# A graph-attention kernel on one core: the last slot as a routine of its own, the first loads in pieces, and the projection's products ahead of q's in the second slot

## The chip, the cores and the metric

The kernel runs on one core of one Trainium2 chip. The metric is the device time of one execution in microseconds (us), lower is better. Times are given as the median of several runs; a profiled execution is one run more, with its own time. Engines are called by the profile's names: PE (TensorE), DVE (VectorE), ACT (ScalarE), POOL (GpSimd), SP (SyncE, which here only issues DMAs); PEld is PE's loading of stationary operands.

## What is computed

Thirty-two graphs of 512 nodes with 512 features each go through two layers. Everything is fp32.

```
x: (32, 512, 512)   adj: (32, 512, 512)
# layer 0: attention with 8 heads of 64, weighted by adj, then residual and layer norm
q, k, v = x @ Wq.T + bq, x @ Wk.T + bk, x @ Wv.T + bv
attn = softmax(q k^T / 8 + log(clip(adj, 1e-8)))
x = layer_norm(x + (attn v) @ Wo.T + bo) * gamma + beta
# layer 1: graph attention with one head
p = x @ fc_w.T + fc_b
l = (p . q_w + q_b) + (p . k_w + k_b)^T ;  l = l + (1 - adj) * (-1e9) ;  l = leaky_relu(l)
out = softmax(l) p + x
```

## The kernel before

**Batches and slots.** The function `fast` works on one graph (batch b) after another. A batch has four slots p = 0 to 3, one for each pair of heads, written by `slot(b, p)`. In each slot PE makes the pair's scores (`score`, L701; ACT takes the exponential, L706), DVE multiplies with the adjacency (`factors`, L714) and adds up the columns (`sums`, L724, L727), and PE multiplies with v (`values`, L739, one slot later). Round this core lies the other work of three batches: q and k of the next pair (`seven_qk`, L540), v of the next batch (`seven_v`), the output projection Wo of the batch before (`seven_wo`, L188) with its layer norm, and layer 1 of the batches before (`dots`, `k_rows`, `softmax`, `eT`, `z`, `out_units`). The q/k, v and Wo products are made with seven half-size products in place of eight (a Strassen-like scheme), so their sums use the same PSUM bank more than once: a bank gets product 1, DVE reads it, and product 6 is added on top.

**Order.** The program order on PE, DVE, ACT and SP is the order in which the code calls things (`manual_schedule`); each engine works through its own queue in that order and waits with semaphores. POOL isn't in that list; it only adds the bias bo to n (L473). So a step that waits holds up all that stands behind it on its engine.

**The second slot (p = 1)** holds, for the batch before, the scaling of the attention's outputs oT 2 and 3 with the reciprocal sums (`scale`, L794), `third_difference` (L808), then four units of `seven_wo` alternating with the units of `seven_qk(b, 2)`, q first, with the second half of `sums` between. Unit 0 of Wo is products 1 and 5, after which DVE writes two differences (L657) and adds bank a to n (L658); unit 1 is products 2 and 6; product 6 is added to bank a. At the slot's start `load_again(b - 1)` fetches x of the batch before as n, and POOL adds bo to it.

```
for i in range(4):
    run(next_qk[i : i + 1])
    if i == 0:
        sums(b, p, 1)
    run(units[i : i + 1])
```

**The start.** x of batch 0, the weights (each one DMA of 1 MB on SP's queue) and the adjacency (16 DMAs) are loaded; PE transposes x (L271), makes q, k and all four units of v, and then enters slot (0, 0). `fold_units` prepares constants of layer 1 in three steps spread over batch 0: `bias` in slot (0, 1), `offset` in (0, 2), `spread` at the end of (0, 3) (L254 to L259). `combine` prepares the sums of weights for the seven products.

**The end.** In slot (31, 3) `load_again(31)`, `load_last_e` (the last adjacency, plain), two leftover `out_units` of batch 29 and `divide_here` (sums over partitions on PE, L817, reciprocals by logarithm and exponential on ACT, refined on DVE, L827 to L833). After the loop stands a tail with layer 1 of batch 30 and what is left of batch 31, ending with `find_range` (a check of the sums' range, L855 to L871) and the outputs.

Of the kernel before, what the change touches and what calls it, by code (L numbers as in the profile page):

```python
# [19 lines left out]
P = 128  # L20
# [10 lines left out]
def kernel(  # L31
# [72 lines left out]
    def load_weight(w, name):  # L104
        w_sb = const.tile([P, DC, D], FP, name=name)
        nc.sync.dma_start(out=w_sb, in_=w.rearrange("(c p) o -> p c o", p=P))
        return w_sb
# [11 lines left out]
    def load_b(dst, src):  # L119
        nc.sync.dma_start(out=dst, in_=src.rearrange("(c p) d -> p c d", p=P))  # L120
# [22 lines left out]
    def load_first_constants():  # L143
        K["wq"] = load_weight(wqT, "wq")
        K["bq"] = load_col(const, bq, "bq")
        K["wk"] = load_weight(wkT, "wk")
        K["bk"] = load_col(const, bk, "bk")
        K["wv"] = load_weight(wvT, "wv")
# [45 lines left out]
    def fold_units(psum, scratch):  # L194
# [56 lines left out]
        def spread():  # L251
            for _, _, part, dg, name, b0 in vectors:
                ps = psum.tile([P, D], FP, tag="m", name=f"ps_{name}")
                nc.tensor.matmul(ps, ones, dg, start=True, stop=True)  # L254
                nc.vector.tensor_copy(K[name], ps)
                ps = psum.tile([P, D], FP, tag="m", name=f"ps_{name}_part")
# [82 lines left out]
    def dots_units(s, small, junk, name):  # L339
# [3 lines left out]
        def unit(c):  # L343
            n = s["n"][:, c, :]
            for u, to in ((K["uk"], s["k"]), (K["uq"], s["q"])):
                nc.vector.scalar_tensor_tensor(  # L346
                    junk, n, 1.0, u, ALU.mult, ALU.mult, accum_out=to[:, c : c + 1]
                )

        def biases():  # L350
            nc.vector.tensor_scalar_add(s["k"], s["k"], K["k0"])
            nc.vector.tensor_scalar_add(s["q"], s["q"], K["q0"])
        return [lambda c=c: unit(c) for c in range(NC)] + [biases]
# [50 lines left out]
    def residual(s):  # L404

        def over(row):
            return row.unsqueeze(1).to_broadcast([P, NC, D])
        nc.vector.tensor_mul(s["yb"], s["n"], over(K["gamma"]))
        nc.vector.tensor_add(s["yb"], s["yb"], over(K["cc"]))
# [9 lines left out]
    def out_units(s, dst, psum, name):  # L419
        def unit(c):  # L420
            pg = psum.tile([P, D], FP, tag="m", name=f"pg_{name}_{c}")
            product(pg, lambda i: s["zT"][:, i, ts(c, P)], lambda i: K["fc"][:, i, :])
            o = s["yb"][:, c, :]
            nc.vector.scalar_tensor_tensor(o, pg, s["r"][:, c : c + 1], o, ALU.mult, ALU.add)  # L424
            nc.sync.dma_start(out=dst[ts(c, P), :], in_=o)
        return [lambda c=c: unit(c) for c in range(NC)]


    def fast(ctx):
# [10 lines left out]
        def load_x(b):  # L440
            s = S[b]
            if b == 0:
                s["n"] = act.tile([P, NC, D], FP, tag="n", name=f"n_{b}")
                load_b(s["n"], x[b])
# [30 lines left out]
        def load_last_e():  # L475
            S[B - 1]["e"] = cT
            load_b(cT, adj[B - 1])
# [6 lines left out]
        def xT(b):  # L484
            s = S[b]
            s["xT"] = act.tile([P, DC, N], FP, tag="xT", name=f"xT_{b}")
            if b == 0:
                return transpose_units(s["n"], s["xT"], ps_m, nc.scalar.copy, f"x_{b}")
            return transposes(s["xT"], s["x"])

# [319 lines left out]
        def divide_here(b, p):  # L810
# [4 lines left out]
            ps = ps_m.tile([P, N], FP, tag="m", name=f"ps_{b}_{p}")  # L815
            for j in range(2):
                nc.tensor.matmul(  # L817
                    ps[j * DK : (j + 1) * DK, :], ones[:, :DK], s["as", p][:, j, :],
                    start=True, stop=True,
                )  # L820
            i = 2 * B - 1 + p % 2
            R = act.tile([P, 2, N], FP, tag="R", name=f"t_{b}_{p}")
            t, r = R[:, 0, :], R[:, 1, :]
            junk = S[b - 1]["w"][:, 0, :]
            nc.scalar.activation(r, ps, AF.Ln)
            nc.scalar.activation(r, r, AF.Exp, scale=-1.0)
            nc.vector.tensor_mul(t, ps, r)  # L827
            nc.vector.scalar_tensor_tensor(
                junk, ps, SUM_MAX, t, ALU.is_le, ALU.mult, accum_out=seen[:, i : i + 1]
            )  # L830
# [382 lines left out]
```

## Time and profile before

| | us |
|---|---|
| median of 3 runs (lowest, highest) | 3574.13 (3572.62, 3574.59) |
| the profiled execution | 3570.67 |
| its span, first to last instruction | 3568.5 |
| PE busy | 3510.2 |
| DVE busy | 2872.7 |
| ACT busy | 1277.6 |
| start of slot (31, 3) | 3439.12 |
| first product of z of batch 31 | 3533.29 |

The granted clock of PE was 0.995 over the span. One batch takes 108.86 us in the middle of the run (the first L658 of batch 3 starts at 361.2 us, that of batch 30 at 3300.0). In a row of the timeline the first two numbers are start and duration in us, "x8" counts instructions, and what stands in brackets is the idle time of the engine ahead of it and what ended it. PE is pipelined, and the ends of its instructions are modelled, so neighbours overlap by some 0.07 to 0.2 us; distances are best read from start to start.

### The profile page before, as it was taken

The numbers are of one execution on the slowest core, as the hardware profiler recorded it, in microseconds if no ns is written. First come the engines' busy times: TensorE is split into PE (matmuls) and PEld (weight loads), VectorE is DVE, ScalarE is ACT, GpSimd is POOL, SyncE is SP. The second block draws the span as 40 slices with busy tenths as digits, with TensorE's granted clock in tenths as the row PEclk, the third lists the DMA queues.
The fourth block names the chain that finished last, engine by engine and source line by source line (L and its number), as shares of the span: only waits on it lengthen the run. The fifth ranks groups of instructions, "written<-read, shape, count | busy, mean of one in ns | idle before, by whom it ended". The sixth has DMA issues, their size and how long they took to land.

```text
span 3568.5 us, 38741 instructions
## 1 busy us (share of the span) xinstructions
PE 3510.2 (98%) x13826; PEld 2040.4 (57%) x13826; DVE 2872.7 (80%) x4708; ACT 1277.6 (36%) x2060; POOL 201.7 (6%) x137
## 2 busy tenths in 40 slices
PE   9999999999999999999999999999999999999988
PEld 3555655655655555556656555555566565565544
DVE  5788878787888888787888888887878888888874
ACT  3334333333333333333343333333333433333332
POOL 0000000000000000000000000000000000000010
PEclk9999999999999999999999999999999999999999
DMA  4344323344233443233442324432334423344220
GB/s 112 48 74 87 54 69 71 66 86 72 60 75 60 80 87 57 68 72 63 86 82 50 75 61 80 86 57 70 74 62 84 86 46 74 65 76 87 51 69 27
DMA packets 880223, 250.68 MB, mean 70 GB/s; under 512 B 807068, under 2 KB 807068, under 8 KB 880024
## 3 DMA queue, kind: packets, MB, share of 16 engines
q1 hardware_dynamic: 880024, 248.15, 35.0%
q8 instruction: 110, 1.80, 0.2%
q14 instruction: 89, 0.73, 0.1%
HBM read 181.93 MB, written 34.65 MB: 61 GB/s over the span
## 4 chain that ended last, share of the span: by engine, by line
PE 95%; DVE 3%; ACT 1%; DMA 0%; issue 0%; SPq 0%; DVEq 0%; ACTq 0%
PE f L540 19%; PE sc L701 13%; PE po L739 12%; PE pz L278 12%; PE pg L278 12%; PE pw_a L188 5%; PE pv_a L188 4%; PE pw_c L188 3%; PE pw_b L188 3%; PE pv_c L188 3%; PE pv_b L188 3%; PE pq L540 2%; PE ps L756 2%; ACT at L706 1%; DVE w L346 0%; DVE at L714 0%
## 5 line engine op out<-in xcount | busy, mean ns | idle before, releaser
L706 ACT ACTIVATE at<-sc 128x1024 f32<-128x1024 f32 x512 | 496.5, 1022 | 892.6 <-PE sc L701 891.3
L714 DVE SCALAR_TENSOR_TENSOR at<-cT,at 128x1024 f32<-128x1024 f32 x512 | 618.3, 1249 | 181.4 <-ACT at L706 181.4
L701 PE MATMUL sc<-qT,kT 64*128 64x512 f32 x2048 | 509.4, 616 | 3.8 <-DVE qT L564 1.9
L739 PE MATMUL po<-at,v 128*64 128x512 f32 x2048 | 469.1, 600 | 1.0 <-DVE at L714 0.9
L278 PE MATMUL pg<-fc,zT 128*128 128x512 f32 x1024 | 445.3, 592 | 1.7 <-DVE yb L424 1.7
L278 PE MATMUL pz<-eT,n 128*128 128x512 f32 x1024 | 446.4, 593 | 0.0
L473 POOL TENSOR_TENSOR n<-n,bo 128x512 f32<-128x512 f32 x128 | 200.7, 1597 | 3262.5 <-PE po L739 1535.8
L701 PEld LDWEIGHTS sc<-qT,kT 64*128 64x128 f32 x2048 | 176.1, 186 | 299.0 <-issue 264.5
L278 PEld LDWEIGHTS pg<-fc,zT 128*128 128x128 f32 x1024 | 194.3, 190 | 234.0 <-issue 217.4
L278 PEld LDWEIGHTS pz<-eT,n 128*128 128x128 f32 x1024 | 195.2, 191 | 230.5 <-issue 220.7
L727 DVE TENSOR_TENSOR as<-as,at 128x1024 f32<-128x1024 f32 x256 | 314.0, 1226 | 5.6
L739 PEld LDWEIGHTS po<-at,v 128*64 128x64 f32 x2048 | 135.7, 137 | 319.2 <-issue 315.0
L540 PE MATMUL f<-T,qk_s 128*128 128x256 f32 x992 | 247.4, 382 | 7.0 <-DVE T L521 3.9
L416 ACT COPY zT<-pz 128x512 f32<-128x512 f32 x128 | 75.0, 586 | 429.3 <-PE pz L278 429.3
L540 PEld LDWEIGHTS f<-T,qk_s 128*128 128x128 f32 x992 | 181.0, 190 | 43.4 <-ACT at L706 5.8
L540 PE MATMUL f<-xT,wq 128*128 128x256 f32 x744 | 194.9, 385 | 8.2 <-ACT at L706 8.2
L747 ACT COPY oT<-po 128x512 f32<-128x512 f32 x128 | 75.2, 588 | 321.6 <-PE po L739 321.6
L540 PEld LDWEIGHTS f<-xT,wq 128*128 128x128 f32 x744 | 137.8, 190 | 53.4 <-ACT at L706 33.9
L724 DVE TENSOR_TENSOR as<-at,at 128x1024 f32<-128x1024 f32 x128 | 154.1, 1204 | 2.2
L794 DVE TENSOR_TENSOR oT<-oT,R 128x512 f32<-128x512 f32 x126 | 128.5, 1061 | 7.5 <-DMA R<-d 7.5
L540 PE MATMUL f<-xT,qk_s 128*128 128x256 f32 x496 | 127.3, 379 | 0.0
L540 PE MATMUL f<-T,wk 128*128 128x256 f32 x496 | 127.3, 379 | 0.0
(212 smaller groups left out, 4710.6 us busy)
## 6 DMA issues: line engine op xcount, KB each, us to landing
n<-in_x_dram SPq DMA_DIRECT2D x32, 1024.0 KB
cT<-in_adj_dram SPq DMA_DIRECT2D x512, 64.0 KB
out_dram<-yb SPq DMA_DIRECT2D x128, 256.0 KB
R<-d SPq DMA_DIRECT2D x126, 256.0 KB
x<-in_x_dram SPq DMA_DIRECT2D x124, 256.0 KB
e<-in_adj_dram SPq DMA_DIRECT2D x31, 1024.0 KB
eP<-e SPq DMA_DIRECT2D x480, 64.0 KB
w<-dk SPq DMA_DIRECT2D x32, 256.0 KB
```

The source lines that it names most:

```text
L188: nc.tensor.matmul(to[:, n, :], right(i, c)[:, ts(n, P)], left[i][:, c, :], start=(first and n == 0 and c == 0), stop=(n == KH - 1 and c = ...
L278: nc.tensor.matmul(ps, lhs(i), rhs(i), start=(i == 0), stop=(i == 3))
L473: nc.gpsimd.tensor_add(s["n"][:, c, :], s["n"][:, c, :], K["bo"])
L540: nc.tensor.matmul(to, left[i][:, c, ts(p, P)], s["B"][i][:, c, :], start=(first and c == 0), stop=(c == KH - 1), skip_group_check=True,)
L701: nc.tensor.matmul(sc[:, j, :], s["kT", p][rows, ts(kc, P)], s["qT", p][rows, :], start=True, stop=True,)
L706: nc.scalar.activation(at, sc, AF.Exp, scale=SCALE)
L714: nc.vector.scalar_tensor_tensor(at, cT[:, kc, :].unsqueeze(1).to_broadcast([P, 2, N]), ADJ_MIN, at, ALU.max, ALU.mult,)
L724: nc.vector.tensor_add(s["as", p], s["at", p, 0], s["at", p, 1])
L727: nc.vector.tensor_add(s["as", p], s["as", p], s["at", p, kc])
L739: nc.tensor.matmul(s["po", p][j * DK : (j + 1) * DK, :], s["v"][h // 4][:, kc, ts(h % 4, DK)], s["at", p, kc][:, j, :], start=(kc == 0), s ...
L747: nc.scalar.copy(s["oT"][p], s["po", p])
L794: nc.vector.tensor_mul(oT, oT, s["R", p][:, k, :])
```

## The change

- **Start:** x of batch 0 and wq come in four DMAs each; `first_xT` transposes x piece by piece into four PSUM banks, and the copies alternate between ACT and DVE. Two of v's four units move behind the q and k products of slot (0, 0). In batch 0 `bias` stands behind all q and k products of its slot, half of wv's combination and all of wo's move, and `spread` moves from the end of slot (0, 3) to slot (1, 0), with both big products ahead of both small ones.
- **Second slot, every batch from 1 on:** the second half of `sums` first, then each unit of `seven_wo` ahead of the unit of `seven_qk` with the same number.
- **Dots:** k's dots and q's are separate lists, in the third slot taken two and two.
- **Last slot:** `last_slot` takes the place of slot (31, 3) and the tail, with a new order of all that is in them; `divide_here` is three steps (add, invert, refine) with banks of the scores' kind; `residual` can work on some of the four rows; `find_range` is two steps, put between z's units; n of batch 31 is loaded in slot (31, 2).

The diff, cut to its core:

```diff
-    def load_weight(w, name):
+    def load_weight(w, name, pieces=1):
-        nc.sync.dma_start(out=w_sb, in_=w.rearrange("(c p) o -> p c o", p=P))
+        load_b(w_sb, w, pieces)
         return w_sb
...
-    def load_b(dst, src):
-        nc.sync.dma_start(out=dst, in_=src.rearrange("(c p) d -> p c d", p=P))
+    def load_b(dst, src, pieces=1):
+        n = 4 // pieces
+        for i in range(pieces):
+            nc.sync.dma_start(
+                out=dst[:, ts(i, n), :],
+                in_=src[ts(i, n * P), :].rearrange("(c p) d -> p c d", p=P),
+            )
 
...
-        K["wq"] = load_weight(wqT, "wq")
+        K["wq"] = load_weight(wqT, "wq", 4)
...
         def spread():
-            for _, _, part, dg, name, b0 in vectors:
+            for _, _, _, dg, name, _ in vectors:
                 ps = psum.tile([P, D], FP, tag="m", name=f"ps_{name}")
                 nc.tensor.matmul(ps, ones, dg, start=True, stop=True)
                 nc.vector.tensor_copy(K[name], ps)
+            for _, _, part, _, name, b0 in vectors:
                 ps = psum.tile([P, D], FP, tag="m", name=f"ps_{name}_part")
                 nc.tensor.matmul(ps[:, :DC], ones, part, start=True, stop=True)
                 nc.vector.tensor_reduce(extra[:, 0:1], ps[:, :DC], AX.X, ALU.add)
...
+        def dot(c, u, to):
+            nc.vector.scalar_tensor_tensor(
+                junk, s["n"][:, c, :], 1.0, u, ALU.mult, ALU.mult, accum_out=to[:, c : c + 1]
+            )
+
+        def bias(to, b0):
+            nc.vector.tensor_scalar_add(to, to, b0)
+        ks = [lambda c=c: dot(c, K["uk"], s["k"]) for c in range(NC)]
+        qs = [lambda c=c: dot(c, K["uq"], s["q"]) for c in range(NC)]
+        return ks + [lambda: bias(s["k"], K["k0"])], qs + [lambda: bias(s["q"], K["q0"])]
...
+    def residual(s, cs=slice(0, 4)):
-            return row.unsqueeze(1).to_broadcast([P, NC, D])
-        nc.vector.tensor_mul(s["yb"], s["n"], over(K["gamma"]))
-        nc.vector.tensor_add(s["yb"], s["yb"], over(K["cc"]))
+            return row.unsqueeze(1).to_broadcast([P, cs.stop - cs.start, D])
+        nc.vector.tensor_mul(s["yb"][:, cs, :], s["n"][:, cs, :], over(K["gamma"]))
+        nc.vector.tensor_add(s["yb"][:, cs, :], s["yb"][:, cs, :], over(K["cc"]))
...
+        ps = {}
+
+        def mul(c):
+            ps[c] = psum.tile([P, D], FP, tag="m", name=f"pg_{name}_{c}")
+            product(ps[c], lambda i: s["zT"][:, i, ts(c, P)], lambda i: K["fc"][:, i, :])
+
+        def add(c):
             o = s["yb"][:, c, :]
-            nc.vector.scalar_tensor_tensor(o, pg, s["r"][:, c : c + 1], o, ALU.mult, ALU.add)
+            nc.vector.scalar_tensor_tensor(o, ps[c], s["r"][:, c : c + 1], o, ALU.mult, ALU.add)
             nc.sync.dma_start(out=dst[ts(c, P), :], in_=o)
-        return [lambda c=c: unit(c) for c in range(NC)]
+        return [(lambda c=c: mul(c), lambda c=c: add(c)) for c in range(NC)]
...
-                load_b(s["n"], x[b])
+                load_b(s["n"], x[b], 4)
...
+        def first_xT():
+
+            s = S[0]
+            s["xT"] = act.tile([P, DC, N], FP, tag="xT", name="xT_0")
+            pt = [ps_m.tile([P, N], FP, tag="m", name=f"pt_x_{i}") for i in range(3)]
+            pt.append(ps_o.tile([P, N], FP, tag="po", name="pt_x_3"))
+            for c in range(NC):
+                for i in range(DC):
+                    nc.tensor.transpose(pt[i][:, ts(c, P)], s["n"][:, c, ts(i, P)], ident)
+            for i in range(DC):
+                (nc.scalar.copy, nc.vector.tensor_copy)[i % 2](s["xT"][:, i, :], pt[i])
...
+            ps = ps_s.tile([P, 2, N], FP, tag="s", name=f"ps_{b}_{p}")[:, 0, :]
+            i = 2 * B - 1 + p % 2
+            R = act.tile([P, 2, N], FP, tag="at", name=f"t_{b}_{p}", bufs=6)
+            t, r = R[:, 0, :], R[:, 1, :]
+
+            def add():
+                for j in range(2):
+                    nc.tensor.matmul(
+                        ps[j * DK : (j + 1) * DK, :], ones[:, :DK], s["as", p][:, j, :],
+                        start=True, stop=True,
+                    )
+
+            def invert():
+                nc.scalar.activation(r, ps, AF.Ln)
+                nc.scalar.activation(r, r, AF.Exp, scale=-1.0)
+
+            def refine():
+                junk = S[b - 1]["w"][:, 0, :]
+                nc.vector.tensor_mul(t, ps, r)
+                nc.vector.scalar_tensor_tensor(
+                    junk, ps, SUM_MAX, t, ALU.is_le, ALU.mult, accum_out=seen[:, i : i + 1]
                 )
+                nc.vector.scalar_tensor_tensor(t, t, 2.0, r, ALU.subtract, ALU.mult)
+                oT = s["oT"][p]
+                nc.vector.scalar_tensor_tensor(oT, oT, -1.0, t, ALU.mult, ALU.mult)
+            return add, invert, refine
...
+            def over_elements():
+                ...
+                pf = ps_m.tile([P, 512], FP, tag="m", name="pf")
+                nc.tensor.transpose(pf[:2, :P], low, ident)
+                nc.vector.tensor_reduce(least, pf[:2, :P], AX.X, ALU.min)
+
+            def over_partitions():
+                one = ps_m.tile([P, 512], FP, tag="m", name="one")
+                nc.tensor.transpose(one[:1, :2], least, ident[:2, :2])
+                ...
+            return over_elements, over_partitions
...
                 if b == 0:
-                    run(combine(K["wv"], K["v_s"]) + combine_qk()[:1])
+                    run(combine(K["wv"], K["v_s"])[:1] + combine_qk()[:1])
                 run(next_qk)
-                units = z(b - 2) if b >= 2 else []
+                units = z(b - 2) if b >= 2 else [spread] if b == 1 else first_v[2:]
                 run(units[:2])
...
                 run(units[2:])
+                if b == 0:
+                    run(combine(K["wv"], K["v_s"])[1:])
...
             if p == 1:
-                units = seven_wo(last, long_banks(last)) if last >= 0 else [bias]
-                for i in range(4):
-                    run(next_qk[i : i + 1])
-                    if i == 0:
-                        sums(b, p, 1)
-                    run(units[i : i + 1])
-                if last >= 0:
+                sums(b, p, 1)
+                if last < 0:
+                    run(next_qk)
+                    bias()
+                else:
+                    units = seven_wo(last, long_banks(last))
+                    for i in range(4):
+                        run(units[i : i + 1])
+                        run(next_qk[i : i + 1])
                     run(stats_units(S[last], small, last))
                     mask(S[last])
             if p == 2:
+                if b == 0:
+                    run(combine(K["wo"], K["wo_s"]))
                 run(next_qk)
...
+                outs = out_units(S[b - 2], out[b - 2], ps_m, b - 2) if b >= 2 else []
                 if b == B - 1:
-                    units, rest = units[:2], units[2:]
-                run(units[:1])
-                dot = dots(last) if last >= 0 else []
-                run(dot[:2])
-                run(units[1:2])
-                run(dot[2:])
+                    load_again(b)
+                    outs, rest = outs[:2], outs[2:]
+                if b == 0:
+                    offset()
+                run_out(outs[:1])
+                ks, qs = dots(last) if last >= 0 else ([], [])
+                run(ks[:2] + qs[:2])
+                run_out(outs[1:2])
+                run(ks[2:] + qs[2:])
                 if last >= 0:
                     k_rows(last)
                 if b < B - 1:
                     sums(b, p, 1)
-                run(units[2:])
+                run_out(outs[2:])
                 divided(b, 0)
                 if b == 0:
-                    run(combine_qk()[1:] + combine(K["wo"], K["wo_s"]))
+                    run(combine_qk()[1:])
...
+        def last_slot():
+            b, last = B - 1, B - 2
+            muls, adds = [m for m, _ in rest], [a for _, a in rest]
+            for kc in (0, 1):
+                score(b, 3, kc)
+            run(values(b, 2))
+            factors(b, 3, 0)
+            sums(b, 3, 0)
+            for kc in (2, 3):
+                score(b, 3, kc)
+            factors(b, 3, 1)
+            load_last_e()
+            vs = values(b, 3)
+            vs[0]()
+            run(muls[:1])
+            run(softmax(last))
+            run(adds[:1])
+            vs[1]()
+            here2, here3 = divide_here(b, 2), divide_here(b, 3)
+            here2[0]()
+            run(muls[1:])
+            nc.vector.tensor_add(S[b]["as", 3], S[b]["as", 3], S[b]["at", 3, 2])
+            run(adds[1:])
+            nc.vector.tensor_add(S[b]["as", 3], S[b]["as", 3], S[b]["at", 3, 3])
+            scale(b, 0)
+            first_difference(b)
+            here2[1]()
+            run(eT(last))
+            for u in here3[:2]:
+                u()
+            here2[2]()
+            here3[2]()
+            zs = z(last)
+            zs[0]()
+            wos = seven_wo(b, other_banks(b))
+            run(wos[:2])
+            new_yb(last)
+            residual(S[last], slice(0, 1))
+            residual(S[last], slice(1, 2))
+            third_difference(b)
+            wos[2]()
+            residual(S[last], slice(2, 3))
+            residual(S[last], slice(3, 4))
+            wos[3]()
+            invert(S[last])
+            run(stats_units(S[b], small, b))
+            run(zs[1:])
+            norm = normalise_units(S[b], small, b)
+            norm[0]()
+            mask(S[b])
+            run(norm[1:])
+            ks, qs = dots(b)
+            run(ks)
+            k_rows(b)
+            run(qs)
+            outs = out_units(S[last], out[last], ps_m, last)
+            soft = softmax(b)
+            run_out(outs[:1])
+            outs[1][0]()
+            soft[0]()
+            outs[1][1]()
+            outs[2][0]()
+            soft[1]()
+            outs[2][1]()
+            run_out(outs[3:])
+            rest_of_layer1(b)
+            zs = z(b)
+            run(eT(b) + zs[:1])
+            range_steps = find_range()
+            range_steps[0]()
+            zs[1]()
+            flag = range_steps[1]()
+            run(zs[2:])
+            run_out(out_units(S[b], out[b], ps_m, b))
+            return flag
...
-        run(xT(0) + qk(0, 0) + v(0))
+        first_xT()
+        first_v = v(0)
+        run(qk(0, 0) + first_v[:2])
...
                 if b == B - 1 and p == 3:
-                    load_again(b)
-                slot(b, p)
-        last = B - 1
...
+                    flag = last_slot()
+                else:
+                    slot(b, p)
         return flag
```

## Prediction, made before the changed kernel was run

> **What bounds the kernel now.** The page first: TensorE (PE) is busy for 98% of the span, and the chain that ended last lies 95% on it.
>
> ```profile
> PE 3510.2 (98%) x13826; PEld 2040.4 (57%) x13826; DVE 2872.7 (80%) x4708; ACT 1277.6 (36%) x2060; POOL 201.7 (6%) x137
> PE 95%; DVE 3%; ACT 1%; DMA 0%; issue 0%; SPq 0%; DVEq 0%; ACTq 0%
> ```
>
> So what can be won is PE's idle 58 us, and what can be lost is any new wait of PE, above all one that repeats with the batch. Next the windows: from 300 to 3400 us PE idles about 0.3 us per batch, and its waits there have one entry, `f L540 <- ACT at L706`, 29 times 0.27 us (second slot, q's products wait for score banks). The other idle time lies at the ends: 6.5 us for the first x, about 12 between 90 and 200 us, and this in the end piece (PE's waits from 3439 us; columns: total, times, longest):
>
> ```profile
> PE ps L817 <- DVE as L727: 7.6, 1, 7.6
> PE pt_e L271 <- ACT cT L396: 7.0, 4, 6.3
> PE pt_e L271 <- ACT e L396: 5.9, 4, 5.2
> PE pg L278 <- DVE yb L424: 1.7, 1, 1.7
> PE po L739 <- DVE at L714: 0.9, 1, 0.9
> ```
>
> Then the one slot that every batch repeats and the change reorders, the second (here batch 20; start, duration), DVE first:
>
> ```profile
> 2196.08 2.36 DVE L714 SCALAR_TENSOR_TENSOR at<-cT,at 128x1024 f32<-128x1024 f32 x2 [5.55 <-ACT at L706]
> 2198.48 1.23 DVE L724 TENSOR_TENSOR as<-at,at 128x1024 f32<-128x1024 f32 x1
> 2199.62 3.45 DVE L794 TENSOR_TENSOR oT<-oT,R 128x512 f32<-128x512 f32 x2
> 2202.99 2.90 DVE L808 TENSOR_TENSOR oT<-oT,oT 128x256 f32<-128x256 f32 x2
> 2205.82 2.35 DVE L714 SCALAR_TENSOR_TENSOR at<-cT,at 128x1024 f32<-128x1024 f32 x2
> 2208.09 0.41 DVE L549 TENSOR_TENSOR qT<-f,qT 128x256 f32<-128x256 f32 x1
> 2208.42 2.47 DVE L727 TENSOR_TENSOR as<-as,at 128x1024 f32<-128x1024 f32 x2
> 2210.81 0.75 DVE L657 TENSOR_TENSOR oT<-oT,t 128x256 f32<-128x256 f32 x2
> 2211.48 0.68 DVE L658 TENSOR_TENSOR n<-pw_a,n 128x512 f32<-128x512 f32 x1
> ```
>
> and PE in the same slot:
>
> ```profile
> 2210.39 1.89 PE L188 MATMUL pw_b<-wo,oT 128*128 128x256 f32 x8
> 2212.22 1.99 PE L188 MATMUL pw_a<-wo_s,oT 128*128 128x256 f32 x8
> ...
> 2220.18 1.13 PE L701 MATMUL sc<-qT,kT 64*128 64x512 f32 x4
> ```
>
> The slot's first score starts at 2193.85; I count from there. DVE has no gap from +2.2 to the end of L658 at +18.31, and PE's product 6 (second pw_a) starts at +18.37, 0.06 after L658's end: it adds to the bank that L658 reads. PE would have been ready at about +18.27. So this place is already on the edge of DVE. The slot ends (next score) at +26.33.
>
> **What the Trainium skill says.** "PSUM — Partial Sum Buffer", PSUM bank collisions: two engines may not be in one bank at once, so software must wait; that is the 0.06 us order above, and it stays. "SBUF — State Buffer", Who interferes with whom: a DVE instruction with two SBUF inputs contends with a GpSimd instruction that reads SBUF. The trace agrees: during GpSimd's four adds n+bo (2199.55 to 2205.61) L794 and L808 take 3.45 and 2.90 us; without them two such scalings took 1.29 (3454.20) and two differences of that shape, L802, 0.75 (3455.41). "TensorE: Matmul & The Clock Gate", Part 1: after an idle window of about 3.4 us, free-running, PE's clock halves. Here four products took 2.05 instead of 1.03 us after a wait of 2.44 us (94.63), but 1.13 after 2.41 (198.52), 1.10 after 1.44: near 2.4 us it is chance, below 1.7 it was never seen.
>
> **1. Second slot, batches 2 to 31.** Removed: the 0.27 us wait for score banks, since Wo's products 1 and 5 need only oT scaled a slot earlier. Moved: q's unit (four products of 0.86) falls behind Wo's first unit, and a second q unit (1.73) falls behind product 6. PE is then ready for product 6 after 1.92+3.58+1.92 (scores, values, scores), 3.45 (Wo 1, 5), 3.45 (q), 1.73 (Wo 2) = +16.05, with 0.1 for the change of form +16.15, instead of +18.27. DVE's queue ahead of L658 loses one instruction only, L549 (0.33 start to start): everything else, the sums L727 too, still stands ahead, and its start hangs on the exponentials of the slot's first scores. L658 ends at +17.98, product 6 starts at +18.04: a new wait of 1.9 us. Behind it on PE: product 6 1.73 (+0.1 as now), q 1.73, Wo 4, 3 3.45, k 0.86, Wo 7 1.73, form 0.08 = 9.68, next score at +27.72. I look for a second wait: k's last add (L568) ends near +26.7, before +27.72; product 4's bank is free at +19.6, needed at +21.5. None. Cost **+1.4 us per batch** (+1.2 if the 0.1s vanish), 30 times: **+42**. GpSimd's load of n is issued where it was, so nothing moves it. In batch 1 n isn't loaded and GpSimd adds nothing there; DVE is early enough, no loss.
>
> **2. The start and batches 0, 1.** x in four pieces: first q product near 7.5 instead of 9.61 (last piece at 6.35 as now, four transposes 0.8, copies on two engines). But wq ends and wk follows at the rate seen (380 GB/s: 2.76 us per MB), wk lands near 11.9, so k starts there instead of 13.05: 1.15 won. Six more DMA issues at 0.5 us push the adjacency's issues 3.1 us back, landing 25.4 instead of 22.3; its reader starts by 26.1, before 32.5 now, since the scores come before half of v; covered. v's second half hides the 0.78 wait at 42.45, bias behind k the 0.84 at 61.28: slot (0,2) starts at 58.0, not 61.28. Then DVE rules: bias 10.2 and factors 4.6 from 58.0, wo's combination (2.65, moved into DVE's gap) to 75.5, then xT, at 76.86 now. From there to the add L549 before at 102.86 it was 26.4 with the combination in it, now 23.8: PE's product there starts at 99.3 instead of 103.32. spread leaves slot (0,3): 111.19 to 117.23, 6.0 with its 2.99 wait. So 10.0 at slot (1,0). There DVE runs without a gap to the copy of uq (about 125.8), next slot 126.0 instead of 135.0: **9.0 won**, less 1 for a clock drop at one of the new waits of up to 2.6: **-8** (5 to 10).
>
> **3. The end.** n(31) is loaded a slot earlier: issue 3432.2, landing +5.6 as in batch 4's second slot, GpSimd's adds 3437.9 to 3443.9 lie on the dots of slot (31,2) (two SBUF inputs, 1.68 instead of 0.69), so DVE's factors start at 3447.6, not 3444.4: PE waits 2.25 for them. PE from 3439.12 to the last z(30): scores 3.84, values 7.43, pg 6.9, sums 1.9, transposes 3.4, pz 13.75, Wo 12.1 = 49.3, with that wait and 1.15 for the third difference (DVE's queue from the softmax at 3456.5 to it sums to 23.3, so 3479.8) 52.7: 3491.85. The waits of 7.6 and 5.9 are gone, covered by pg, transposes and z. Now ACT copies zT first (0.7), then the normalising factors 1.5, mask 1.15, four k dots 3.05, turn 0.2: 3498.45; round trip of the k row 5.75 (3516.43 to 3522.23 before): 3504.2; softmax to first pz 11.06 (3522.23 to 3533.29 before): 3515.3, 18.0 earlier. q's dots and pg (to 3506.4) lie beside it. Last: find_range's first step now stands on PE behind the first pz. It needs the residual (4.57 after the out DMA, 2.2) and seven small DVE steps, low at 3520.7, pz ends at 3518.75: 1.95 of wait and 0.4, against 0.88 now: 1.4 back. **-16.6** (10 to 22).
>
> **Costed at nothing.** The k dots ahead of q's and the split of out_units into product and add issue the same instructions in nearly the same places while q's and k's results are needed only after both. The second half of wv's combination waits for v's products in batch 0, 0.68 us in a stretch where DVE waits for exponentials (4 us ahead of its old place at 47.05); without that cover 0.7 once. On SP, n(31)'s load stands ahead of the k row's and the output's DMAs and waits for the last q products (3432.2), all of those come after 3437; the reload of cT stands ahead of one output and waits for the last factors (3453.4), and its reader comes 40 us later. The row of reciprocals for oT 0 and 1 lands 9.6 us after its issue began (3444.48 to 3454.1 before), now about 3457.2, its scaling comes at 3462.8: if DVE were earlier, this would be late next.
>
> **Sum.** 42 - 8 - 16.6 = +17.4 on the profiled execution's 3570.67 (span 3568.5 and 2.17 around it): 3588. The median of the runs shown is 3.46 above it, so **3591**.
>
> **Rivals.** (a) Faster: product 6 doesn't wait, because DVE gets to L658 by +16.1. Against it: DVE's queue has no gap. For it: GpSimd's adds cost DVE 4.3 us in this slot, and were they to fall elsewhere DVE would be there. Then 30 x -0.28 = -8.4 and 3574 - 8.4 - 8 - 16.6 = 3541. The sign turns where the slot costs 24.6 / 30 = 0.8, that is L658 0.6 earlier than I say; chance 0.13, and 0.06 for between, near 3572. (b) The new wait of 1.9 halves the clock each time: 1.8 more (2.05 + 1.80 against 1.03 twice at 94.63), 30 times 54: 3645. Only waits over 2.4 did so here: 0.07. (c) The end gains a third: DVE, whose queue there has no slack, is later by what GpSimd and the split residual cost, -6: 3602; chance 0.12. (d) Likeliest, 0.62: 3591, own range 3580 to 3603.
>
> **Numbers.** A measurement tells about 0.2%, 7 us, from no change: 3567 to 3581 is the same. Faster 0.15 (a and part of between), same 0.10 (the low edge of d and between), slower 0.75. Range 3570 to 3613: (d), (c), most of between, with the start's and the end's bounds; (a) and most of (b) left out.
>
> **What would show it.** A wait `pw_a L188 <- DVE n L658` of about 1.9 us, 30 times, and none of f on `at L706`; batch period 110.25 instead of 108.86; slot (1,1) near 126; z(31) starting 18 us before the old place, counted from slot (31,3). Wrong if the period falls, or the products behind L658 run at half clock.

## The result, and the profile after

The changed kernel takes 3589.49 us (median of 5 runs, 3588.78 to 3591.19), the kernel before 3574.13: a ratio of 1.0045, with a 95% interval of 1.003 to 1.006. It is **slower** by 15 us, 0.45%; 3591 had been predicted. The profiled execution of after took 3588.78 us with a span of 3587.0, so its span is 18.5 longer than that of before (17.4 predicted). In the kernel after, L658 has become L678, L549 L569, L714 L734, L727 L747, L794 L814, L808 L828, L188 L193, L540 L560, L739 L759, L701 L721 and L278 L284.

The page first, busy time and the chain of work that ended last:

```profile
PE 3506.0 (98%) x13826; PEld 2040.6 (57%) x13826; DVE 2885.3 (80%) x4716; ACT 1275.7 (36%) x2058; POOL 199.0 (6%) x137
PE 81%; DVE 14%; issue 3%; ACT 1%; DMA 1%; SPq 0%; DVEq 0%; ACTq 0%
```

PE has as much to do as before. What moved is the chain: DVE's share went from 3% to 14%, so PE now waits for DVE at a place that repeats. The waits of PE name it (columns: total us, times, longest us):

```profile
PE pw_a L193 <- DVE n L678: 51.3, 30, 1.8
PE pt_e L277 <- ACT cT L401: 5.1, 4, 4.4
PE f L560 <- DVE qT L569: 4.8, 2, 2.4
...
PE po L759 <- DVE at L734: 2.4, 1, 2.4
...
PE pf L893 <- DVE low L891: 0.9, 1, 0.9
```

The first line is the cost: 30 waits, one for each batch from 2 on, with the 31 waits of f for score banks gone. The waits for cT, at and low are what is left in the end piece; those of 7.6 and 5.9 are gone. The wait for qT, in batches 0 and 1, was there before and has grown from 3.1 to 4.8 us. The second slot of batch 20 again, first DVE (start, duration):

```profile
2219.82 2.36 DVE L814 TENSOR_TENSOR oT<-oT,R 128x512 f32<-128x512 f32 x2
2222.10 2.90 DVE L828 TENSOR_TENSOR oT<-oT,oT 128x256 f32<-128x256 f32 x2
2224.92 3.42 DVE L734 SCALAR_TENSOR_TENSOR at<-cT,at 128x1024 f32<-128x1024 f32 x2
2228.27 2.47 DVE L747 TENSOR_TENSOR as<-as,at 128x1024 f32<-128x1024 f32 x2
2230.66 0.76 DVE L677 TENSOR_TENSOR oT<-oT,t 128x256 f32<-128x256 f32 x2
2231.33 0.69 DVE L678 TENSOR_TENSOR n<-pw_a,n 128x512 f32<-128x512 f32 x1
```

and PE (in brackets the idle time ahead of the row and what ended it):

```profile
2228.48 1.89 PE L193 MATMUL pw_b<-wo,oT 128*128 128x256 f32 x8
2232.07 1.99 PE L193 MATMUL pw_a<-wo_s,oT 128*128 128x256 f32 x8 [1.70 <-DVE n L678]
...
2241.76 1.99 PE L721 MATMUL sc<-qT,kT 64*128 64x512 f32 x8
```

DVE goes without a gap from L814 to L678. Its sums (L747) end at 2230.7, only then come the differences and L678, and product 6 starts 0.05 after L678's end. From the products ahead of it to product 6 it is 3.59 us, where products follow each other after 1.73 elsewhere in the slot: 1.86 lost. GpSimd's adds now lie partly on the factors (L734 takes 3.42 for two, not 2.36) instead of on L814; their cost to DVE together is as before. The slot takes 27.71 us (2214.05 to 2241.76), the period of a batch is 110.25 (before 108.85).

In three pieces, by starts of scores, the span's difference is:

| from, to | before | after | difference | predicted |
|---|---|---|---|---|
| start, slot (1,1) | 135.00 | 126.59 | -8.4 | -9 |
| slot (1,1), slot (31,3) | 3304.12 | 3349.46 | +45.3 | +42, +1 for the clock |
| slot (31,3), end of the span | 129.38 | 110.95 | -18.4 | -16.6 |

The prediction's -8 for the start held 1 us for a drop of PE's clock to half; it stands in the second row here, where the drops fell.

### The profile page after: what moved, and what is told of

The parts are those of the page before. It is cut to its first block, busy times and chain, and to the rows that moved or that the text cites. A ratio compares the mean times of both kernels' runs of the same rounds, so it can differ in the third digit from the quotient of the medians.

```text
span 3587.0 us, 38723 instructions
## 1 busy us (share of the span) xinstructions
PE 3506.0 (98%) x13826; PEld 2040.6 (57%) x13826; DVE 2885.3 (80%) x4716; ACT 1275.7 (36%) x2058; POOL 199.0 (6%) x137
## 4 chain that ended last, share of the span: by engine, by line
PE 81%; DVE 14%; issue 3%; ACT 1%; DMA 1%; SPq 0%; DVEq 0%; ACTq 0%
PE f L560 16%; PE pz L284 12%; PE pg L284 11%; PE sc L721 11%; PE po L759 9%; DVE at L734 5%; PE pv_a L193 4%; PE pw_a L193 3%; PE pv_c L193 3%; PE pv_b L193 3%; DVE oT L814 2%; DVE oT L828 2%; PE pq L560 2%; PE ps L776 2%; PE pw_c L193 2%
## 5 line engine op out<-in xcount | busy, mean ns | idle before, releaser
L734 DVE SCALAR_TENSOR_TENSOR at<-cT,at 128x1024 f32<-128x1024 f32 x512 | 619.7, 1251 | 174.6 <-ACT at L726 174.6
L721 PE MATMUL sc<-qT,kT 64*128 64x512 f32 x2048 | 510.5, 617 | 0.8 <-DVE qT L584 0.5
L759 PE MATMUL po<-at,v 128*64 128x512 f32 x2048 | 468.1, 599 | 2.4 <-DVE at L734 2.4
L284 PE MATMUL pz<-eT,n 128*128 128x512 f32 x1024 | 446.2, 593 | 0.0
L284 PE MATMUL pg<-fc,zT 128*128 128x512 f32 x1024 | 445.5, 592 | 0.2 <-DVE yb L433 0.2
L721 PEld LDWEIGHTS sc<-qT,kT 64*128 64x128 f32 x2048 | 176.5, 186 | 296.3 <-issue 267.7
L284 PEld LDWEIGHTS pg<-fc,zT 128*128 128x128 f32 x1024 | 194.3, 190 | 233.3 <-issue 216.4
L284 PEld LDWEIGHTS pz<-eT,n 128*128 128x128 f32 x1024 | 194.7, 190 | 231.2 <-issue 221.3
L759 PEld LDWEIGHTS po<-at,v 128*64 128x64 f32 x2048 | 135.4, 136 | 320.0 <-issue 316.5
L747 DVE TENSOR_TENSOR as<-as,at 128x1024 f32<-128x1024 f32 x254 | 308.1, 1213 | 5.5
L560 PE MATMUL f<-T,qk_s 128*128 128x256 f32 x992 | 245.7, 380 | 8.0 <-DVE qT L569 4.8
L560 PEld LDWEIGHTS f<-T,qk_s 128*128 128x128 f32 x992 | 185.4, 190 | 38.3 <-DVE qT L569 5.6
L560 PE MATMUL f<-xT,wq 128*128 128x256 f32 x744 | 190.9, 379 | 0.0
L560 PEld LDWEIGHTS f<-xT,wq 128*128 128x128 f32 x744 | 138.3, 190 | 22.3
L572 ACT ACTIVATE qT<-f,bq 128x256 f32<-128x256 f32 x124 | 58.8, 474 | 234.8 <-PE f L560 234.8
L581 ACT ACTIVATE qT<-f,bq 128x256 f32<-128x256 f32 x124 | 58.8, 474 | 210.5 <-PE f L560 210.5
L814 DVE TENSOR_TENSOR oT<-oT,R 128x512 f32<-128x512 f32 x126 | 127.6, 1054 | 1.0 <-DMA R<-d 1.0
```

The costliest lines, as they stand in the source:

```text
L284: nc.tensor.matmul(ps, lhs(i), rhs(i), start=(i == 0), stop=(i == 3))
L560: nc.tensor.matmul(to, left[i][:, c, ts(p, P)], s["B"][i][:, c, :], start=(first and c == 0), stop=(c == KH - 1), skip_group_check=True,)
L721: nc.tensor.matmul(sc[:, j, :], s["kT", p][rows, ts(kc, P)], s["qT", p][rows, :], start=True, stop=True,)
L734: nc.vector.scalar_tensor_tensor(at, cT[:, kc, :].unsqueeze(1).to_broadcast([P, 2, N]), ADJ_MIN, at, ALU.max, ALU.mult,)
L747: nc.vector.tensor_add(s["as", p], s["as", p], s["at", p, kc])
L759: nc.tensor.matmul(s["po", p][j * DK : (j + 1) * DK, :], s["v"][h // 4][:, kc, ts(h % 4, DK)], s["at", p, kc][:, j, :], start=(kc == 0), s ...
```

## The experiments

**Theory:** the three parts add up, each as its own. The second slot costs 1.4 us per batch, because the sums stand ahead of L678 on DVE and PE has nothing left to do before L678 is done; the start and the end win. **First rival:** the wait is GpSimd's doing, whose adds lengthen DVE's work; then the order of DVE's queue is of little account. **Second rival:** the parts lean on each other (the new start or the new end lose or win only beside the new slot).

**The three parts apart.** The first kernel is the changed one with the second slot's old order:

```diff
-                sums(b, p, 1)
                 if last < 0:
+                    sums(b, p, 1)
                     run(next_qk)
                     bias()
                 else:
                     units = seven_wo(last, long_banks(last))
                     for i in range(4):
-                        run(units[i : i + 1])
                         run(next_qk[i : i + 1])
+                        if i == 0:
+                            sums(b, p, 1)
+                        run(units[i : i + 1])
```

> The changed kernel with the second slot of batches 1 to 31 in its old order (q's unit, then the sums, then Wo's unit), all else as changed. Theory (the loss is the wait of Wo's product 6 for DVE's L678, 30 times 1.4 us net, while start and end gain some 25 us): batch period back to 108.86 us, waits of 0.27 us of q's products for the exponentials back, total 3589.5 - 30 x 1.395 - 1.3 (batch 1) = 3546 us, faster than both kernels. Rival (the loss comes from the new last slot or the start, and the wait only shifts): 3580 to 3590 us.

The second is the kernel before with nothing but the new order in that slot (the same lines the other way round).

> The kernel before with nothing changed but the order in the second slot of batches 1 to 31. Theory: 30 new waits of 1.7 us at product 6, period 110.25 us, total 3574.1 + 30 x 1.395 = 3616 us. Rival (the order costs only together with the other parts): within 10 us of 3574.

Two more have the kernel before with the new last slot alone (the first of these kernels with the start's edits undone), and with the new start alone.

> The kernel before with the new last slot (and n of batch 31 loaded in slot (31, 2)) alone: start, batches 0 and 1 and the second slot in the old order. Theory: from the start of slot (31, 3) to the end of the span 111 instead of 129.4 us, all else equal: 3573 - 18.4 = 3555 us. Rival (part of the gain at the end is only the start's lead carried on, or the end is worth less by itself): above 3560.

> The kernel before with the new start alone (x and wq in four loads, v's second half later, bias, combinations and spread moved). Theory: slot (1, 1) starts near 126.6 instead of 135.0 us, and one or two drops of PE's clock behind the remaining waits of DVE give back up to 3 us: 3573 - 5 to 8 = 3565 to 3568 us. Rival (the gain is lost again in batch 1 or 2, where DVE is late anyway): within 2 us of 3573.

| kernel | us | the kernel before on the same chip | ratio, 95% interval |
|---|---|---|---|
| old order in the second slot, rest changed | 3547.43 | 3573.01 | 0.993 (0.9913 to 0.9946) |
| new order alone | 3614.15 | 3573.01 | 1.0116 (1.0099 to 1.0133) |
| new last slot alone | 3556.30 | 3573.84 | 0.9952 (0.9936 to 0.9969) |
| new start alone | 3565.66 | 3573.84 | 0.9976 (0.9969 to 0.9984) |

The parts alone make +41.1, -17.5 and -8.2, together +15.4, and the whole change makes +15.4. Start and end together make -25.6, alone -25.7. That they meet within 0.1 us is luck: the interval of each difference is 3 to 6 us either way. Beyond that nothing shows of the parts leaning on each other: with the new order alone the period is 110.25 as in the whole change, and with the new start alone or the end alone it stays between 108.84 and 108.86. The second rival falls. The list of PE's waits of the kernel with the new order alone begins with the same entry (its line numbers are those of before):

```profile
PE pw_a L188 <- DVE n L658: 51.2, 30, 1.7
```

and in the one with the old order it has gone, and the wait for score banks is back:

```profile
PE f L560 <- ACT at L726: 8.2, 31, 0.3
```

**Two ways to take the wait away.** In the first the sums stand one unit later, behind Wo's second unit, with the new order otherwise kept:

```diff
-                sums(b, p, 1)
                 if last < 0:
+                    sums(b, p, 1)
                     run(next_qk)
...
                         run(units[i : i + 1])
+                        if i == 1:
+                            sums(b, p, 1)
                         run(next_qk[i : i + 1])
```

> The changed kernel with Wo's units still ahead of q's, but the second half of the sums (2.47 us on DVE) moved from ahead of Wo's unit 0 to behind its unit 1. Theory (product 6 waits because DVE has the sums queued ahead of the read of bank a): the read ends 2.47 us earlier, at about +15.5 of the slot, before PE is ready at +16.15; no wait at product 6 and none of q's products, slot 26.33 - 0.5 = 25.8 us, period 108.3 us, total 3589.5 - 30 x 1.9 = 3532 us, the fastest of all. Rival 1 (the order q behind Wo is wrong in itself, or a later step, product 4's bank or k's last add, becomes late by the moved sums): period stays above 108.86 and the total above 3547. Rival 2 (the read is late because of GpSimd's adds, the sums don't matter): 3589.

In the second, GpSimd's adds of bo are left out in the changed kernel (so the bias of the output projection is missing from the result), and DVE's queue stays as it is:

```diff
-            for c in range(NC):
-                nc.gpsimd.tensor_add(s["n"][:, c, :], s["n"][:, c, :], K["bo"])
```

> The changed kernel without GpSimd's four additions of bo to n in each batch; this leaves out the bias bo. Theory: scaling and third difference take 2.0 instead of 6.3 us, DVE reads bank a 4.3 us earlier, no wait at product 6, period 108.3 us; in the last slot PE's 2.4 us wait for the factors goes too: total 3589.5 - 57 - 2 = 3530 us. Rival (DVE's slow stretch isn't caused by GpSimd): the scaling and the difference stay at 6 us and the total at 3589 us.

Measured: 3532.21 us with the sums later (ratio 0.9887, 0.987 to 0.9903) and 3526.03 without the adds (0.9867, 0.985 to 0.9883); 3532 and 3530 had been expected. Both have a period of 108.27. With the sums later, batch 20's second slot on DVE:

```profile
2189.92 3.42 DVE L734 SCALAR_TENSOR_TENSOR at<-cT,at 128x1024 f32<-128x1024 f32 x2
...
2193.94 0.68 DVE L678 TENSOR_TENSOR n<-pw_a,n 128x512 f32<-128x512 f32 x1
...
2198.40 2.48 DVE L747 TENSOR_TENSOR as<-as,at 128x1024 f32<-128x1024 f32 x2
```

and on PE:

```profile
2193.47 1.89 PE L193 MATMUL pw_b<-wo,oT 128*128 128x256 f32 x8
2195.20 1.89 PE L193 MATMUL pw_a<-wo_s,oT 128*128 128x256 f32 x8
```

GpSimd still costs DVE as much (3.42), but L678 ends at +15.6 of the slot (which starts at 2179.04) and product 6 follows with no wait at +16.16, where it had been computed to be ready. Without the adds, DVE's rows of the same slot (start 2177.34; lines are 2 lower) are

```profile
2183.11 1.29 DVE L812 TENSOR_TENSOR oT<-oT,R 128x512 f32<-128x512 f32 x2
2184.32 0.75 DVE L826 TENSOR_TENSOR oT<-oT,oT 128x256 f32<-128x256 f32 x2
...
2190.42 0.68 DVE L676 TENSOR_TENSOR n<-pw_a,n 128x512 f32<-128x512 f32 x1
```

so the add to n ends at +13.8 with the sums still ahead of it. Theory and first rival are therefore both half right: DVE has 1.9 us too much ahead of L678. The sums are 2.4 of it, and GpSimd's adds lengthen the rest by 4.3 (1.1 on L814, 2.15 on L828, 1.06 on L734); taking away either is enough. Taking away both, which was not run, should bring the middle no more, since PE then has no wait left there. Of the 4.1 us between the two spans (3529.8 and 3525.7), 1.7 are a clock drop of batch 0 that only the first of them had. The other 2.4 lie behind the start of slot (31,3): up to the first pz 4.5 are won without the adds, where the wait of 2.40 for the factors and a clock drop behind it are gone, and after it 2.1 are lost, where PE waits 1.97 for low instead of 0.7 and a clock drop follows.

**The end's two remaining waits.** Two kernels start from the one with the sums later. In one, each step of `find_range` stands one unit of z later (`zs[1]` ahead of the first, `zs[2]` ahead of the second):

> The variant with the sums later, and find_range's two steps one pz unit later (behind the second and the third). Theory: PE's wait of 0.7 to 1.3 us for low at the first step is gone, since low comes 2 us after the first pz unit and the second lasts 3.43; from the first pz of batch 31 to the end of the span about 1 us less. Rival (the wait only shifts to another place of the end): the same distance.

3530.47 us in a single run. The wait for low is gone (in the timeline of PE, pf has no bracket):

```profile
3494.31 7.84 PE L284 MATMUL pz<-eT,n 128*128 128x512 f32 x16
3501.99 0.27 PE L893 MATMUL pf<-ident,low 128*2 128x128 f32 x1
```

From the first pz to DVE's last add it is 28.88 us (3494.31 to 3523.19) instead of 30.03 in the changed kernel (3552.02 to 3582.05) and in the one with the sums later: 1.1 won. To the end of the span 0.65 of it is left (34.38 against 35.03 with the sums later). In the other, the load of n for batch 31 stands at the start of the last slot, where it was before the change:

> The variant with the sums later, and n of batch 31 loaded at the start of the last slot, where it was before. Theory (PE's 2.4 us wait for the factors in the last slot is the dots' loss to GpSimd's adds): that wait is gone, the dots of slot (31, 2) take 0.69 each, and GpSimd's adds slow another stretch of DVE some 10 to 20 us later, where DVE's queue sets the pace up to the third difference but z covers it: last slot to end 0 to 2 us shorter. Rival (the factors wait for something else): the 2.4 us stay.

3533.20 us in a single run: nothing won. The wait of 2.4 for the factors is gone, as expected, but PE has two others:

```profile
3440.99 1.08 PE L842 MATMUL ps<-as,ones 128*64 128x512 f32 x4 [0.87 <-DVE as L1088]
...
3447.42 1.99 PE L193 MATMUL pw<-wo,oT 128*128 128x256 f32 x8 [1.73 <-DVE w L854]
```

GpSimd's adds now lie on sums (L1088: 2.05 for one of 128 x 1024 where 1.22 is usual) and on the scaling of oT (L814: 3.44 for two). From slot (31,3) to the end of the span it is 112.57 us, against 112.53 with the load early. But 1.7 of the 112.53 are a clock drop behind the wait for the factors; the changed kernel's trace has the same wait without the drop and takes 110.95. So the wait moves with the adds, and which place costs less depends on whether the clock drops; one run of each doesn't settle it.

**The start's parts.** Both kernels start again from the one with the sums later, and ran once each. In the first, x and wq come in one load each:

> The kernel is e3_sums_later with x of batch 0 and wq in one DMA each, as before the change. The prediction held that x's last piece lands when the whole did, and that the k product waits for wk's landing in any case, so that the pieces win only the time from the first q product's old start to its new one less what k waits: 1.15 us. Then slot (1,1) starts about 1.1 us later than in e3_sums_later (128.9), and the time is 3531 to 3535. Rival: with q the first products start 1.7 us later and all of it reaches the end, 1.7 or more. Second rival: nothing, since from slot (0,2) on DVE sets the pace and has slack ahead of it; then slot (1,1) starts where it did.

3534.94 us. The first product of q starts at 10.06 instead of 7.43, slot (0,2) at 60.38 instead of 59.48, and slot (1,1) at 129.78 instead of 128.86: 0.9 of the 2.6 us reach the end of the start, as the theory has it, since k's products wait 0.87 for wk in the kernel with the pieces and not at all here. What else the time lost is a clock drop (1.65 us in slot (1,1)). But the traces with four loads reach slot (0,2) anywhere from 58.84 to 61.27 us, according to when the loads land, and 60.38 lies among them: this pair leans to the theory, and doesn't rule out either rival. In the second, `spread` stands at the end of slot (0,3) again:

> The kernel is e3_sums_later with the step spread back at the end of slot (0,3), in its new inner order. Theory: with nothing beside it, the step keeps PE from slot (1,0) for about 6 us, of which 3 is waiting; in slot (1,0) PE then has less to do but its wait for DVE is no longer there, so slot (1,1) starts 2 to 4 us later than in e3_sums_later (128.9). Rival: the place of the step is of no account, since DVE, which runs without a gap to slot (1,1), sets that slot's start; then slot (1,1) starts at the same time within 1 us.

3537.29 us, and slot (1,1) starts at 135.83, 7.0 later than with the move: more than the theory's 2 to 4, and its rival falls. 1.2 of it is there at slot (0,2) already (60.68; here x's last transposes wait another 1.08 us for their load) and has nothing to do with the move. The rest, 5.8, is `spread`, which keeps PE for 6.24 us (111.29 to 117.53) and ends in a wait that takes the clock along:

```profile
117.01 0.59 PE L263 MATMUL ps_uk_part<-fold_more,ones 128*128 128x4 f32 x2 [3.72 <-DVE uq L260]
117.53 3.79 PE L721 MATMUL sc<-qT,kT 64*128 64x512 f32 x8
```

From the slot's first scores to its second it is 8.67 us instead of 6.49, and its last step waits 1.37 for DVE: slot (1,0) lasts 18.30 us without `spread` in it against 18.52 with it. The theory had left out the drop, which makes 2.2 of the 5.8. The kernel before had a drop in the same slot (117.23 to 125.38, 8.15 us between its scores). So the move makes the greater part of the start's 8.4 us. The other moves at the start (v's second half, `bias`, the combinations) were not tried apart.

**The best version**, sums later and `find_range` later, measured in several runs:

> The kernel is e7_range_later again (the change, with the second half of the sums behind the second unit of Wo, and each step of the range's check one unit of z later), now measured in rounds. The theory sums to the change's time less 30 x 1.98 us in the middle and 0.6 us at the end, with 1 to 3 us of clock drops either way: 3528 to 3533, a ratio to the kernel before of about 0.988.

3527.98 us against 3573.67 on the same chip, ratio 0.9869 (0.9852 to 0.9885): 1.7% below the changed kernel's median and 1.3% below the kernel before. It is the changed kernel with three calls moved. Against the one with the sums later, the medians (of two chips) differ by 4.2 us and the traces by 2.8: about 1 by the move of `find_range`, and 1.7 by one clock drop less. The rest is open.

## Why the prediction was right, step by step

**Second slot: right in mechanism and size.** Product 6 was computed to be ready at +16.15 and to start at +18.04; it started at +18.02, and at +16.16 where nothing holds it. The next score was predicted at +27.72 and came at +27.71; the period is 110.25 both ways. Before, it was 108.85 by the two starts of L658 given with the profile before (361.2 and 3300.0), not 108.86, so the slot cost 1.40 per batch, 30 times that is 42.0, and 42 had been predicted. No second wait came, as was said.

**The rest of the middle: a term was mis-sized.** 45.3 less 42.0 leaves 3.3 where 1 was allowed for clock drops. Two drops make it: in slot (1,1) the scores and values ran 1.67 longer (7.17 from its first to its second scores, 5.50 in the best version), and after the wait for `L569` in batch 1 the products cost 1.7 more (9.66 to the next scores, 7.96 in before at the same place).

**The start: right, with a slip of 0.5.** Slot (0,2) came at 58.84 (58.0 predicted), the product behind `L569` at 100.10 (99.3), slot (1,0) at 108.07 (107.2), slot (1,1) at 126.59 (126.0). The 0.8 is there from slot (0,2) on. The three terms that the prediction names for it, 1.15, 0.78 and 0.84, take 61.28 to 58.5, not to 58.0. The other 0.4 is the start of k's products at 12.30 instead of 11.9, since wk landed later than the rate gave. The term "k starts when wk has landed" was right (PE waits 0.70 for wk). In the eight traces with all of the new start, slot (1,1) comes between 126.59 and 128.86, against 135.00 to 137.84 in the three with the old one.

**The end: right, with one term too dear and a drop that stayed away.** Slot (31,3) to the first pz was 18.2 shorter (18.0 predicted), with waits of 2.39 for the factors (2.25) and 0.99 for the third difference (1.15). The mis-sized term is `find_range`'s: 1.4 us were to be given back, and 0.5 were (first pz to DVE's last add: 29.57 before, 30.03 after). PE's timeline after:

```profile
3552.02 4.46 PE L284 MATMUL pz<-eT,n 128*128 128x512 f32 x8
3557.42 0.27 PE L893 MATMUL pf<-ident,low 128*2 128x128 f32 x1 [0.94 <-DVE low L891]
```

low came 5.40 after the first pz, as computed, but the eight products ahead take 4.46, not 3.45: after the wait of 4.37 for the transposes they start at half clock, and that loss, which the working forgot, lies under the wait for low. (Before, the same loss stood open: 32 products of pz took 14.71 us to the start of what follows, against the working's 13.75.) Another 0.7 was won in the time from DVE's last add to the end of the span (5.64 before, 4.95 after), which no part of the change touches; with the range's check later it was 5.50.

**The sum: partly luck.** The three pieces missed by +0.6, +2.3 and -1.8 us, and these nearly cancel. The piece at the end leans on chance most. In the seven other traces with the wait of 2.4 to 2.6 us for the factors, a clock drop of 1.7 us follows it, and in this one it doesn't; with it, the end would have won 16.7, as predicted. And the step from the profiled execution to the median added 3.46 us because that of before lay so far below its median; that of after lies 0.71 below.

**The rivals.** The faster case needed L678 before +16.1, and named GpSimd's adds as what would bring it there; without them L678 ends at +13.8 and the time is 3526, below its 3541, since the middle wins 0.58 per batch and not 0.28: small delays beside the lost wait go as well (before, the first units of q are 0.96 and 0.92 apart, not 0.86, and product 6 stands 1.83 from its neighbours, not 1.73). At the end the wait for the factors goes too. The forecast gave this case 0.13 for the kernel as it stands, and it didn't come. The half clock after each wait of 1.9 didn't come either: the products of q behind product 6 start 0.86 apart. The end won more than the prediction, not only a third of it.

## What to carry to other kernels

When products are moved ahead on an engine that bounds the kernel, the work that frees their banks must be moved ahead too, on the other engine's queue: count what stands ahead of the releasing instruction there, not only whether that engine has time on the whole. A wait of 1.7 us that repeats 30 times outweighed 26 us won at the two ends, and one call moved behind that place gave back more than it had cost (57 us against 41). Judge a change of several parts by kernels with each part alone: here they added up within the noise.

## What was not expected of the hardware

**Whether a wait halves PE's clock depends on when it falls.** In the two rows of PE that follow, after and then before, the wait is the same, and only the first is followed by half clock (1.99 us for four products, not 1.13):

```profile
191.50 1.99 PE L560 MATMUL f<-T,qk_s 128*128 128x256 f32 x4 [2.41 <-DVE qT L569]
```

```profile
198.52 1.13 PE L540 MATMUL f<-T,qk_s 128*128 128x256 f32 x4 [2.41 <-DVE qT L549]
```

The traces keep the granted clock. In each of them the stretches at half clock last 3.41 us or a multiple of it (but for the last, which the trace's end cuts), and their starts lie multiples of 3.41 apart: in after 126.77 and 191.63, 19 times 3.41. "TensorE: Matmul & The Clock Gate" of the Trainium skill, Part 1, says that the window in which the clock is judged runs freely; the traces agree. So a trace can be cut into its windows. Here are the two around each wait, first after, then before (stretch, length, PE busy; the column PEclk is the granted clock):

```profile
core 0: us, PE busy (x) PEld busy (x) DVE busy (x) ACT busy (x) POOL busy (x), PEclk, DMA share, GB/s
188.22:191.63 3.41, 1.00 (x6) 0.54 (x5) 3.41 (x6) 0.00 (x0) 0.00 (x0) 1.00 1.19 145
191.63:195.04 3.41, 3.41 (x9) 2.69 (x10) 2.68 (x10) 2.67 (x5) 0.00 (x0) 0.50 0.76 118
```

```profile
193.59:197.00 3.41, 2.52 (x12) 1.88 (x10) 3.38 (x4) 0.79 (x2) 0.00 (x0) 1.00 1.20 215
197.00:200.41 3.41, 1.89 (x9) 1.69 (x10) 3.23 (x8) 1.31 (x3) 0.00 (x0) 1.00 0.86 120
```

In after all of the wait lies in one window, and the next one is at half clock; in before it is split over two, and neither is. The wait for L569 in batch 0, 2.38 or 2.39 us, is in ten traces: in the four where 2.05 us or more of it fell into one window the clock dropped, in the six where it was 1.97 or less it didn't. The 30 waits of 1.7 in the middle leave at most 1.75 us of idle time in a window and never dropped it, in after and in the new order alone. No sharp limit is shown: at other places windows with 1.8 to 2.0 us of idle time went either way. The page names an idle time of about 3.4 us, as the prediction quoted; here 2.05 was enough. A drop of 3.41 us costs PE half of that where it has no other wait, 1.7 us; one more or less of them is part of the 1 to 3 us between traces whose work is the same.

**A drop came after a wait of only 1.2 us.** In slot (1,1) four small products with pauses between them and a wait of 1.21 stand ahead of the scores. In the changed kernel:

```profile
126.28 0.39 PE L263 MATMUL ps_uk_part<-fold_more,ones 128*128 128x4 f32 x2 [1.21 <-DVE uq L260]
126.59 3.65 PE L721 MATMUL sc<-qT,kT 64*128 64x512 f32 x8
```

In the trace of the best version the scores took 1.99 after the same wait (126.87), while the earlier single run of that same kernel took 3.45 (126.59): the kernel doesn't decide it. Of nine traces with this step, the five with the whole wait in one window dropped, and the four with it split didn't. The prediction had said that no wait below 1.7 was seen to do so. In after that window holds 2.06 us of PE's work, 0.78 of it the four small products. If products of 4 columns counted for nothing, the window would be idle for 2.13 us, as in the drops above; that is argued from these sums and was not tried by itself.

**What GpSimd costs DVE, by operation.** Beside its adds of 128 x 512, two DVE scalings of 128 x 512 with both inputs in SBUF took up to 3.45 instead of 1.29, two differences of 128 x 256 2.90 instead of 0.75, and one dot of 128 x 512 1.56 to 1.66 instead of 0.69. Four adds cost DVE 4.3 us in the second slot, before and after, though they fall in part on other instructions. That agrees with "SBUF — State Buffer" of the Trainium skill, Who interferes with whom, by which a DVE instruction with two inputs in SBUF contends with a GpSimd instruction that reads SBUF.
